# An LSTM's last steps and the attention after it: where one group's statistics and eight accumulating loads are issued

## The chip, the cores and the metric

The kernel runs on one core of one Trainium2 chip. The metric is the device time of one execution in microseconds (us). The engines are TensorE (PE in the profile), VectorE (DVE), ScalarE (ACT), GpSimd (POOL) and SyncE (SP), which here issues DMAs only.

## The reference

The input x is 128 batches of 64 nodes of 256 features, 8192 tokens in all. Four layers follow each other, and each adds its result to x:

```
for layer in (L0, L1, L2, L3):
    x = x + layer(relu(layernorm(x)))
L0: two graph convolutions with adj (64 x 64), then for p = 1..4 an LSTM over
    windows of p consecutive nodes; its last h replaces the window's last node
L1: attention with 4 heads of 64 over the 64 nodes of a batch, masked where adj == 0
L2: graph convolution, then linear, batchnorm, relu, linear, batchnorm
L3: three graph convolutions with adj * adj, 256 -> 512 -> 1024 -> 256
```

The change lies where L0 ends and L1 begins: `x = x + L0(...)`, the layer norm of the new x, and the first attention groups.

## The kernel before, in words

**Groups.** The tokens form NG = 16 groups of 512. The residual x of a group is a tile `xs[g]` of 128 partitions by 4 by 256 (512 KB). Groups 0 to 3 stay resident. Groups 4 to 7 and 8 to 11 are loaded from DRAM into memory that held the state of the LSTM, by `x_for(0)` and `x_for(1)` (L259, four loads each through `load_x`, L58, on SP's queue). Groups 12 to 15 are loaded in attention.

**The LSTM's state.** It is kept with features on the partitions, in four tiles `hs[0]` to `hs[3]` of 32 batches each, four groups to a tile. When a tile is final, `turn_nodes(part, room)` (L274) transposes a quarter of its nodes on VectorE (L278) and puts it down in DRAM (`ys`, L283, four DMAs on SP's queue). Then `add_turned(g)` (L287) adds a group's values to `xs[g]` with one accumulating DMA that POOL issues (L291).

**The last steps.** For window length p = 4 the units of work are taken in pairs; the pair at j = 2 is the last one. Each unit takes steps t = 1, 2, 3, and the two units alternate, so that there are six steps, and the code numbers them `slot` 0 to 5. A step (`next_step`, L677) makes four differences on VectorE (L685 to L690) and then two gate sets. A gate set (`seven`, L170) is a form of Strassen's scheme with seven products on PE (L568) in four PSUM banks: the results of the first two are copied by ScalarE (L179, L180) and summed by VectorE (L182, L183), POOL sums two of them (L187), VectorE makes the other outputs (L193, L197), and ScalarE applies the gates (L582). The step ends with the cell state (L699, L700), a tanh (L601) and the hidden state on VectorE (L603; in a unit's last step L609). `next_step` returns this last VectorE instruction, which the loop keeps as `stepped`.

Beside the six steps, both parts of `turn_nodes` for `hs[0]` and `hs[1]`, the accumulating loads listed for each slot in `ADDED_BESIDE` (L165), and `x_for` are issued. `summed_last()` is POOL's latest sum (L187); a load stands behind it on POOL.

**The first attention group.** At slot 4 the layer norm of group 0 is made as well: `ln_relu` makes statistics on VectorE (L92, L94, L95), a power on POOL (L96), the shift on VectorE (L98) and four activations on ScalarE (L111). Then `transposed` turns h on PE (L127) and `features` copies it (L302) and makes differences (L306, L310, L311).

**Attention.** For each group PE makes values (L901), the queries and keys in a scheme of seven products (L879, with POOL's sum at L187 again), transposes the exponentials of the group before (L962), attends (L975), transposes h of the next group (L127) and makes the scores (L926). `normalized(g + 2)` (L853) makes the layer norm of the group two ahead: statistics on VectorE (L860, L862), two operations on POOL (L864, L866). `add_output` (L983) adds the result of the group before the last to x on POOL (L990). In groups 1 to 3 and from 5 on, `add_turned` is called once in a group behind an operation that POOL made for a layer norm (`shifts_made`, L866).

**What sets the order.** A scheduler orders each engine's instructions by its own estimate of time, with program order as priority. `with tc.issue_after(ins)` puts the instructions of its block behind `ins` on the engine of `ins`; it is an order on that engine alone. Each engine runs its instructions in the order that results. The eight PSUM banks (`psp`) are taken in turn by all matmuls.

Of the kernel before, what the change touches and what calls it, by code (L numbers as in the profile page):

```python
# [24 lines left out]
NK = PER  # L25
# [13 lines left out]
def adj_preln_kernel(ctx: ExitStack, tc: tile.TileContext, x_in, adj, vec, bg0, bg1,  # L39
# [122 lines left out]
    HN = GN // 2  # L162

    sums_on_pool = []
    ADDED_BESIDE = ((), (), (0,), (1,), (2,), (3, 4))  # L165

    def summed_last():
        return sums_on_pool[-1]
# [90 lines left out]
    def x_for(i):  # L259

        four = hx.tile([P, PER, GT, D], F32, tag=f"h{i}", name=f"x_for_h{i}")
        for k in range(PER):
            xs.append(four[:, k])
            load_x(xs[-1], len(xs) - 1)
# [49 lines left out]
    with tc.tile_pool(name="lw", bufs=5) as lw:  # L314
# [220 lines left out]
        with tc.tile_pool(name="back", bufs=1, reuse_waits="tile") as back_pool, \  # L535
# [176 lines left out]
            def blocks_of(p, wi, wh):  # L712
# [14 lines left out]
                return ws, lambda: make([3])  # L727


            w0 = first_blocks(  # L730
                w_next[0], lw.tile([P, 2, 1024], F32, tag="w", name="s"), copied_of[5:9]
            )
            for p, nk in ((1, 8), (2, 8), (3, 7), (4, 8)):
                n = nk * HB
                wi, wh = w_next
                if p < 4:
                    w_next = (load_w(wih, p), load_w(whh, p))
                starts = range(0, NODES // p // nk * nk, nk)
                units = [(tiles, k0) for tiles in ((0, 1), (2, 3)) for k0 in starts]

                for j in range(0, len(units), 2):
                    two = [unit(p, *u, nk) for u in units[j : j + 2]]
                    first_steps(p, n, two, units[j : j + 2], w0)
                    if p > 1:
                        flush()
                        if j == 0:
                            ws, last_sum = blocks_of(p, wi, wh)
                    if j + 2 == len(units):
                        if p < 4:
                            w0 = first_blocks(  # L750
                                w_next[0], weight_tile(),
                                [copied_of[i] for i in (9, 14, 15, 15)] if p == 1 else None,
                            )
                        else:
                            w_att = weight_tile()
                            nc.sync.dma_start(
                                out=w_att[:, :, 0:768], in_=wqkv.rearrange("(c p) f -> p c f", p=P)
                            )
                            wqk = [[w_att[:, c, m * D : (m + 1) * D] for c in range(2)] for m in range(2)]
                            wv = w_att[:, :, 512:768]  # L760
                            ss = [w_att[:, c, 768:1024] for c in range(2)]
                            nc.vector.tensor_tensor(ss[0], wqk[1][0], wqk[1][1], ALU.add)
                            nc.vector.tensor_tensor(ss[1], ss[0], wqk[0][0], ALU.subtract)
                            nc.vector.tensor_tensor(wdiff, wqk[0][0], wqk[1][0], ALU.subtract)
                    for t in range(1, p):
                        for i, u in enumerate(two):
                            stepped = next_step(
                                t, p, n, u, ws, last_sum if (j, t, i) == (0, 1, 0) else None
                            )

                            if p == 4 and j == 2:
                                slot = 2 * t + i - 2
                                if slot == 0:
                                    room = keep.tile([P, 2, TN, 2, 32], F32, tag="arena", name="turned")
                                for part in range(2 * slot, min(2 * slot + 2, 8)):
                                    turn_nodes(
                                        part,
                                        room[:, part % 3] if part % 3 < 2 else back_pool.tile(
                                            [P, TN, 2, 32], F32, tag="hc", name="turned"
                                        ),  # L780
                                    )()
                                for x_of_group in ADDED_BESIDE[slot]:
                                    with tc.issue_after(summed_last()):
                                        add_turned(x_of_group)
                                if slot > 2:
                                    if slot < 5:
                                        x_for(slot - 3)
                            if p == 4 and j == 2 and t == p - 1 and i == 0:

                                h = back_pool.tile([P, GT, D], F32, tag="hc", name="h")  # L790
                                with tc.issue_after(stepped):
                                    ln_relu(xs[0], h)
                                hTs = keep.tile([P, 2, 2, GN], F32, tag="arena", name="hT")
                                hT = features(transposed(h))
# [55 lines left out]
    with tc.tile_pool(name="att", bufs=2, reuse_waits="tile") as ap_:  # L850
# [151 lines left out]
        for g in range(NG):  # L1002
            if g == NG - NK + 1:
                turn_pool.__exit__(None, None, None)
                hres_pool.__exit__(None, None, None)
                with tc.using_default_side("right"):
                    ar_right = ctx.enter_context(
                        tc.tile_pool(name="arena_r", bufs=NG // 2, reuse_waits="tile")
                    )
            hT_all, blocks = hT  # L1010
            v = ap_.tile([P, 2 * GT, P], F32, tag="v", name="v")
            moved = values(hT_all, v, (0,))
            if 0 <= g - NK < NK:
                with tc.issue_after(moved):
                    load_x(xs[g + 2 * NK], g + 2 * NK)
            q, k, finish = queries_keys(blocks)
            if g == 0:
                h = normalized(1)
            if last is not None:
                with tc.issue_after(finish.behind):  # L1020
                    if g > 1:
                        add_output(g - 2, pss, ri)
                    sums_of()
            if last is not None:
                e, ri, v_last = last
                if g > 1:
                    eT, turned = turn(e)
            added = finish()
            if g == NG - 1:

                w1 = w_att[:, :, 0:512]
                w2 = w_att[:, :, 512:1024].rearrange("p a (b f) -> a p b f", f=D)
                nc.sync.dma_start(out=w1, in_=w1t.rearrange("(c p) f -> p c f", p=P))
            moved = values(hT_all, v, (1,))
            if put_down:
                with tc.issue_after(moved):
                    put_down()
            put_down = None
            if g == 1:

                eT, turned = turn(e)
            if 0 < g <= NG - NK:
                with tc.issue_after(shifts_made[g]):
                    if g < 4:
                        add_turned(g + NK)
                    elif g > 4:
                        add_turned(g + NK - 1)
            if g + 1 < NG:
                hT = features(transposed(h))
            if g == 0:  # L1050

                with tc.issue_after(last_copy.ins):
                    nc.scalar.activation(rsum, mhalf[:, 0:1], AF.Exp)
            if g == NG - 1:
                turned_in = mixed(0, (on_scalar, on_scalar))
            if last is not None:
                pss = attend(eT, v_last)
            e_next = []

            def masked_scores():  # L1060
                e, masked = scores(q, k)
                e_next.append(e)
                return masked

            if g < NG - 1:
                masked_scores()
            else:
                with tc.issue_after(turned_in), tc.issue_after(added):
                    activated(ar_right, 1, masked_scores)
            ri_next, sub, sums_of = softmax(e_next[0])  # L1070
            last = (e_next[0], ri_next, v)
            with tc.issue_after(sub):
                if g < 8:
                    put_down = turn_nodes(
                        g + 8, tp.tile([P, TN, 2, 32], F32, tag="turned", name="turned")
                    )
                if g + 2 < NG:
                    h = normalized(g + 2)
                elif g + 2 == NG:
                    activated(ar_right, 0)  # L1080
# [587 lines left out]
```

## Time and profile before

| what | value |
|---|---|
| median of 3 runs (lowest to highest) | 2465.1 us (2464.9 to 2465.72) |
| the profiled execution, its own time | 2465.76 us |
| its span | 2464.0 us |
| mean granted clock of TensorE | 0.997 |
| PE busy | 2431.4 us (99%) |
| DVE busy | 1544.5 us (63%) |
| ACT busy | 1128.6 us (46%) |
| POOL busy | 463.3 us (19%) |

The time of an execution is a little more than its span, here by 1.76 us. Busy is the sum of an engine's instructions; an engine's idle time matters only where the work that ends last waits for it. In the timeline of this execution a step of the LSTM lasts 24.17 us on PE; slot 3 starts at 1133.08 us, slot 4 at 1157.25, the products of the last step at 1194.06, and attention at 1219.92.

### The profile page before, as it was taken

What the parts mean: (1) busy time and instruction counts of PE and PEld (TensorE: products, weight loads), DVE (VectorE), ACT (ScalarE), POOL (GpSimd) and SP (SyncE); (2) the same over time, 40 slices, a digit from 0 to 9 for tenths busy, and PEclk for the clock granted to TensorE, in tenths of its full rate; (3) what the DMA queues carried; (4) which work ended last, traced back from release to release, by engine and by line L of the source; (5) the groups of instructions that cost most, each with busy time, mean ns of one, the idle gap of its engine ahead of it and who ended that gap; (6) DMA issues with size and microseconds to landing.
All of it is one profiled execution on the core that took longest, in us unless ns stands there. A gap on an engine that the chain in (4) does not pass through costs nothing.

```text
span 2464.0 us, 46585 instructions
## 1 busy us (share of the span) xinstructions
PE 2431.4 (99%) x19564; PEld 2074.0 (84%) x19564; DVE 1544.5 (63%) x2768; ACT 1128.6 (46%) x2026; POOL 463.3 (19%) x400
## 2 busy tenths in 40 slices
PE   9999999999999999999899999999999999999999
PEld 6678888889999998888788864486888898898888
DVE  6668866666566565576499886476556455454544
ACT  4557754444354343343455566564333323333332
POOL 4431211111111111111134431023111111101110
PEclk9999999999999999999899999999999999999999
DMA  3200000001000000152257310010133100000000
GB/s 127 93 2 1 1 18 1 1 1 35 1 1 1 1 1 1 18 98 52 33 98 138 74 40 2 1 60 10 27 61 61 27 10 19 10 10 10 18 10 18
DMA packets 161587, 73.20 MB, mean 30 GB/s; under 512 B 104417, under 2 KB 157793, under 8 KB 161377
## 3 DMA queue, kind: packets, MB, share of 16 engines
q1 hardware_dynamic: 147712, 56.82, 9.3%
q0 software_dynamic: 12672, 12.58, 3.4%
q8 instruction: 154, 2.52, 0.4%
q10 hardware_dynamic: 992, 0.82, 0.1%
q14 instruction: 57, 0.46, 0.1%
HBM read 40.84 MB, written 20.97 MB: 25 GB/s over the span
## 4 chain that ended last, share of the span: by engine, by line
PE 88%; DVE 7%; ACT 3%; POOL 1%; issue 1%; DMA 0%; DVEq 0%; POOLq 0%; ACTq 0%
PE ps L568 41%; PE ps L1455 16%; PE ps L1503 8%; PE ps L829 4%; PE ps L144 4%; PE ps L1419 2%; PE ps L511 2%; PE ps L487 2%; PE ps L879 2%; PE ps L1211 2%; PE ps L1262 2%; PE ps L901 1%; ACT arena L237 1%; POOL arena L187 1%; DVE hT L306 1%
## 5 line engine op out<-in xcount | busy, mean ns | idle before, releaser
L568 PE MATMUL ps<-diff,s 128*128 128x256 f32 (+1 forms) x1824 | 393.5, 371 | 0.9 <-DVE diff L689 0.9
L1455 PE MATMUL ps<-arena 128*128 128x256 f32 x1792 | 392.4, 380 | 0.0
L1455 PEld LDWEIGHTS ps<-arena 128*128 128x128 f32 x1792 | 337.9, 190 | 53.9 <-issue 9.2
L568 PEld LDWEIGHTS ps<-diff,s 128*128 128x128 f32 x1824 | 346.1, 190 | 33.9 <-issue 1.6
L582 ACT ACTIVATE gates<-gates,lbias 128x512 f32<-128x512 f32 (+5 forms) x426 | 244.3, 621 | 203.8 <-DVE gates L193 146.0
L187 POOL TENSOR_TENSOR gates<-p 128x512 f32<-128x512 f32 (+1 forms) x115 | 149.2, 1297 | 892.5 <-DVE p L183 841.6
L568 PE MATMUL ps<-h,w 128*128 128x256 f32 (+1 forms) x1028 | 242.7, 373 | 0.0
L568 PE MATMUL ps<-diff,w 128*128 128x256 f32 (+1 forms) x1040 | 238.7, 370 | 0.0
L568 PEld LDWEIGHTS ps<-diff,w 128*128 128x128 f32 x1040 | 197.4, 190 | 18.2
L568 PEld LDWEIGHTS ps<-h,w 128*128 128x128 f32 x1028 | 196.2, 191 | 19.6 <-issue 0.5
L582 ACT ACTIVATE gates<-ps,lbias 128x256 f32<-128x256 f32 (+3 forms) x213 | 91.8, 477 | 249.2 <-PE ps L568 249.1
L187 POOL TENSOR_TENSOR arena<-arena 128x256 f32<-128x256 f32 (+1 forms) x73 | 81.8, 1120 | 580.4 <-DVE arena L183 550.7
L237 ACT ACTIVATE arena<-arena 128x512 f32<-128x512 f32 (+1 forms) x160 | 88.7, 582 | 186.9 <-POOL arena L187 94.6
L1503 PE MATMUL ps<-arena 128*128 128x128 f32 x1280 | 149.7, 276 | 0.0
L193 DVE TENSOR_TENSOR gates<-p,ps 128x512 f32<-128x512 f32 (+1 forms) x115 | 76.2, 663 | 114.4 <-PE ps L568 114.2
L1503 PEld LDWEIGHTS ps<-arena 128*128 128x128 f32 x1280 | 145.5, 192 | 1.1
L193 DVE TENSOR_TENSOR arena<-arena,ps 128x256 f32<-128x256 f32 (+1 forms) x73 | 43.5, 596 | 156.4 <-PE ps L1455 87.4
L182 DVE TENSOR_TENSOR p<-p,ps 128x512 f32<-128x512 f32 (+1 forms) x131 | 86.7, 662 | 53.9 <-PE ps L568 53.1
L568 PE MATMUL ps<-state,w 128*128 128x256 f32 (+1 forms) x512 | 116.1, 370 | 0.9 <-ACT p L179 0.8
L197 DVE TENSOR_TENSOR gates<-p,ps 128x512 f32<-128x512 f32 (+1 forms) x115 | 76.5, 666 | 64.4 <-PE ps L568 63.8
L568 PE MATMUL ps<-state,s 128*128 128x256 f32 (+1 forms) x512 | 115.8, 369 | 0.0
L829 PE MATMUL ps<-arena,w 128*128 128x512 f32 x256 | 114.3, 599 | 0.0
(207 smaller groups left out, 4027.4 us busy)
## 6 DMA issues: line engine op xcount, KB each, us to landing
x<-in_x SPq DMA_DIRECT2D x19, 512.0 KB, 5.4
y<-turned SPq DMA_DIRECT2D x64, 128.0 KB, 3.5
v<-vt SPq DMA_DIRECT2D x128, 64.0 KB, 2.5
w<-in_wih SPq DMA_DIRECT2D x4, 1024.0 KB, 8.5
x_for_h<-in_x SPq DMA_DIRECT2D x8, 512.0 KB, 9.2
x<-y POOLq DMA_DIRECT2D x8, 512.0 KB, 6.4
x_for_h<-y POOLq DMA_DIRECT2D x8, 512.0 KB, 6.5
z<-w SPq DMA_DIRECT2D x64, 64.0 KB, 2.0
```

The source lines that it names most:

```text
L144: last = nc.tensor.matmul(pss[b][half * 64 : half * 64 + 64, c, t, :], lhsT=src[rows, t, col : col + 64], rhs=a2[rows, :], start=True, sto ...
L182: nc.vector.tensor_tensor(p1, p1, ps[2], ALU.add)
L187: nc.gpsimd.tensor_tensor(out=out[1][1], in0=p1, in1=p5, op=ALU.add).ins
L193: nc.vector.tensor_tensor(out[0][1], p1, ps[1], ALU.add)
L197: last = nc.vector.tensor_tensor(to, p, q, ALU.add)
L237: nc.scalar.activation(o, o, func)
L487: nc.tensor.matmul(ps[:, t, :], lhsT=m0[:, c, tok : tok + P], rhs=wg[0][:, c, :], start=(c == 0), stop=(c == 1),)
L568: nc.tensor.matmul(ps[:, r], lhsT=wc[:, j, :], rhs=bc, start=first and r == 0 and c == 0, stop=True, skip_group_check=True,)
L582: nc.scalar.activation(o, ps, func, bias=lbias[:, col : col + 1])
L829: nc.tensor.matmul(ps, lhsT=w1[:, c, m * P : (m + 1) * P], rhs=a[:, 2 + c, :], start=(c == 0), stop=(c == 1),)
L1455: nc.tensor.matmul(ps[:, r, :], lhsT=w[:, c, col : col + P], rhs=b[:, c, :], start=first and r == 0 and c == 0, stop=c == 1, skip_group_ch ...
L1503: nc.tensor.matmul(ps[:, t, :], lhsT=w[:, c, t * P : (t + 1) * P], rhs=b[:, c, :], start=first and t == 0 and c == 0, stop=c == 3, skip_gr ...
```

## The change

It has three parts. The statistics of the first attention group are put behind the last VectorE instruction of the step before (`stepped_before`, slot 3) instead of that of slot 4. The accumulating loads of groups 0 to 7 are listed in pairs beside slots 2 to 5; before, groups 0, 1 and 2 were listed one by one beside slots 2 to 4, groups 3 and 4 beside slot 5, and groups 5 to 7 were loaded in attention groups 1 to 3. And `x_for(0)` and `x_for(1)` are called at slots 2 and 3 instead of 3 and 4.

```diff
-    ADDED_BESIDE = ((), (), (0,), (1,), (2,), (3, 4))
+    ADDED_BESIDE = ((), (), (0, 1), (2, 3), (4, 5), (6, 7))
...
+            stepped = None
...
                         for i, u in enumerate(two):
+                            stepped_before = stepped
                             stepped = next_step(
...
                                 for x_of_group in ADDED_BESIDE[slot]:
                                     with tc.issue_after(summed_last()):
                                         add_turned(x_of_group)
-                                if slot > 2:
-                                    if slot < 5:
-                                        x_for(slot - 3)
+                                if slot in (2, 3):
+                                    x_for(slot - 2)
                             if p == 4 and j == 2 and t == p - 1 and i == 0:
...
-                                with tc.issue_after(stepped):
+                                with tc.issue_after(stepped_before):
                                     ln_relu(xs[0], h)
...
             if 0 < g <= NG - NK:
                 with tc.issue_after(shifts_made[g]):
-                    if g < 4:
-                        add_turned(g + NK)
-                    elif g > 4:
+                    if g > 4:
                         add_turned(g + NK - 1)
```

## The prediction

> **What bounds the kernel now.** I read the page first, then the chain of waits around the change, then each engine's timeline from 1100 to 1350 us, then a table of stretches. The page says that TensorE works nearly all the time, so only the places where it stands still can give time back; the clock row shows one weak slice, the 20th, which is 1170 to 1232 us.
>
> ```profile
> PE 2431.4 (99%) x19564; PEld 2074.0 (84%) x19564; DVE 1544.5 (63%) x2768; ACT 1128.6 (46%) x2026; POOL 463.3 (19%) x400
> PEclk9999999999999999999899999999999999999999
> ```
>
> The timeline of PE there shows the hole. Columns: start, length, line, operands, count, and in brackets the idle time before it and its releaser.
>
> ```profile
> 1179.69 1.89 PE L568 MATMUL ps<-diff,w 128*128 128x256 f32 x8
> 1192.10 2.16 PE L127 MATMUL ps<-ident,h 128*128 128x128 f32 x8 [10.52 <-ACT h L111]
> 1194.06 3.58 PE L568 MATMUL ps<-h,w 128*128 128x256 f32 x8
> ...
> 1229.42 1.04 PE L127 MATMUL ps<-ident,h 128*128 128x128 f32 x8
> ```
>
> The last products of step five of six (slot 4 in the code) are issued by 1181.42 (1179.69 and eight at 0.216 us, the spacing of every full run of eight). PE's next instructions are the transposes of the first attention group's h, ahead of the last step's products, and they wait 10.52 us. They then take 1.96 us start to start instead of 1.03, and the eight after them 3.41 instead of 1.73. The other engines show why h is late:
>
> ```profile
> 1186.82 1.29 DVE L609 TENSOR_TENSOR h<-gates 128x512 f32<-128x512 f32 x2 [1.18 <-ACT gates L601]
> 1188.04 1.40 DVE L92 BATCH_NORM_STATS2 st<-x 128x6 f32<-128x256 f32 x4
> ...
> 1190.18 1.04 POOL L96 TENSOR_TENSOR rstd<-rstd,mhalf 128x4 f32<-128x4 f32 x1 [10.35 <-DVE rstd L95]
> ...
> 1191.45 2.07 ACT L111 ACTIVATE h<-x,nmr,rstd 128x256 f32<-128x256 f32 x4 [4.66 <-DVE nmr L98]
> ```
>
> The statistics (L92) start exactly when slot 4's last VectorE instruction (L609) is done. Data does not hold them: the accumulating load of xs[0] was issued at 1130.21 us and such a load lands 5.9 to 8.7 us after issue, by 1140. It is the order that the old tie asks for.
>
> A second, smaller loss lies in attention. For groups 2 and 4 (POOL, DVE, PE, then POOL and DVE):
>
> ```profile
> 1256.08 1.32 POOL L291 DMA_DIRECT2D x_for_h<-y  x1
> 1256.92 3.01 POOL L990 TENSOR_TENSOR x<-x,o 128x512 f32<-128x512 f32 x2
> 1259.40 1.75 POOL L187 TENSOR_TENSOR k<-p 128x512 f32<-128x512 f32 x1
> ...
> 1259.69 2.02 DVE L306 TENSOR_TENSOR hT<-hT 128x512 f32<-128x512 f32 x1 [0.81 <-ACT hT L302]
> ...
> 1261.21 0.69 PE L926 MATMUL ps<-k,q 64*64 64x64 f32 x32 [0.67 <-POOL k L187]
> ...
> 1286.38 1.28 POOL L187 TENSOR_TENSOR k<-p 128x512 f32<-128x512 f32 x1
> ...
> 1290.07 0.69 DVE L306 TENSOR_TENSOR hT<-hT 128x512 f32<-128x512 f32 x1 [0.81 <-ACT hT L302]
> ```
>
> With an accumulating load (L291) ahead of them, POOL's sums come about 3 us later, meet L306 and stretch it from 0.69 to 2.02, and PE waits for k. The table of stretches cuts attention at each group's first values matmul; columns after the stretch are its length and each engine's busy time:
>
> ```profile
> 1246.53:1261.83 15.30, 14.15 (x193) 11.94 (x188) 14.31 (x29) 8.06 (x14) 6.32 (x6) 1.00 0.66 116
> 1261.83:1277.03 15.20, 14.16 (x195) 11.94 (x189) 14.26 (x28) 8.06 (x14) 6.33 (x6) 1.00 0.61 106
> 1277.03:1291.31 14.28, 13.92 (x194) 11.84 (x189) 13.30 (x29) 8.06 (x14) 4.95 (x5) 1.00 0.53 110
> 1291.31:1305.14 13.83, 13.81 (x194) 11.90 (x189) 12.90 (x28) 7.96 (x14) 6.10 (x6) 1.00 0.56 116
> ```
>
> These are groups 2 to 5. Groups 2 and 3 have the load in front; group 4 has none, but starts late; group 5 has it behind POOL's sums and is bound by PE alone: 13.83.
>
> **What the Trainium skill says.** "TensorE: Matmul & The Clock Gate", section "What's actually happening": an idle window of about 3.4 us halves PE's clock, and about as much work restores it. The trace agrees: after 10.52 us idle, the next 5.37 us hold work that takes 2.70 at full pace, and the granted clock of 1181.42 to 1194.06 is 0.59. "SBUF — State Buffer", section "Who interferes with whom": a VectorE instruction with two SBUF inputs and a GpSimd one that reads SBUF lock each other out. L306 at 2.02 beside L187, and 0.69 without, agrees. "DMA: Bandwidth & Descriptors", section "SWDGE vs HWDGE vs iDMA": accumulating transfers go only through GpSimd, which writes their descriptors. Agrees: each costs POOL 1.3 us.
>
> **The change, part by part.**
>
> *The tie.* The statistics may start after slot 3's last VectorE instruction (L603, over at 1163.88) instead of slot 4's (1188.1). From first L92 to last L111 takes 1188.04 to 1193.52, 5.5 us. Now VectorE has slot 4's own work around it (4.7 us between 1163.79 and 1168.5) and ScalarE is busy 9.33 of the 24.17 us; with 4.7 and 4 us added h is ready by about 1178, before 1181.42. VectorE is busy 13.57 us of that slot, so 2.0 us of statistics fit. Saved: the last step then starts at 1181.42 + 0.97 (eight transposes at full clock, as at 1360.92) = 1182.39, lasts 24.17 as slot 4 does, and attention's first matmul comes at 1206.56 instead of 1219.92: **13.36 us**. What is late next: nothing; slot 5's differences (L685 to L690) were done by 1168, and of the eight PSUM banks the last of slot 4's second gate set is free at 1182.31 (L197), while the product that may need it comes 5.2 us into the step.
>
> *The new wait.* L98 on VectorE waits for POOL's power (L96), 0.83 us in the trace. Behind it could stand slot 4's L183, which ended at 1165.68 and frees a bank that PE uses again at 1167.61. Four L92, the rest and the wait could make it 3 us late, PE 1 us; if the order puts L183 first, nothing. Not shown by the trace: 0 to 1.5 us lost, a gain excluded. I take 0, since a wait behind ready work is the likelier order.
>
> *Pairs of loads.* L291 is added once in each of slots 2, 3 and 4, none in slot 5, and gone from groups 1 to 3: eight in either kernel. A pair in slot 5 took POOL from 1216.98 to 1219.61, and POOL idles some 10 us before each L187 of these steps; VectorE's L193 inside that pair took its usual 0.69. Cost nothing, hidden by POOL's idle time; without that cover, 1.3 us each. DMA is busy 0.12 to 0.15 there. The pair with xs[0] lands by about 1144, 20 us before use.
>
> *SP's queue.* The two groups of four loads (L58) come one slot earlier in the text. Today they run at 1100.0 to 1108.8, behind 21 puts, and land by 1119.5. If four of them pass eight puts, y[1] is complete 5 us later, about 1111; loads 4 and 5 are issued at 1178. Nothing. Bounds: 0 either way.
>
> *Attention.* Group 1 (14.99 us) has its waits for VectorE and ScalarE, not POOL's sum: 0. Group 2 keeps its late start and becomes like group 4: 15.30 to 14.28, 1.02. Groups 3 and 4 become like group 5: 1.37 and 0.45. Together **2.84 us**. Bounds: 0, if another wait takes over, and 4.0, if group 1 also falls to 13.83.
>
> Sum: 13.36 + 2.84 = 16.2 us. The profiled execution has a span of 2464.0 and 1.76 around it (2465.76); 2465.76 - 16.2 = 2449.56, and it lies 0.66 above the median of the runs, so 2448.9: I say **2449.0**.
>
> **The rivals.**
> *Attention gives nothing* (0.14): VectorE is busy 14.3 of group 2's 15.3 us, so another of its waits may take over. Against it: groups 4 and 5 run the same work without the load in front. Time 2451.7.
> *h is still late* (0.08): PE works in order; if the transposes stand between slot 4's two gate sets (1169.34), h, ready at 1169.4 to 1178, stalls PE 4 us at mid value, and 2.8 us of slow clock follow. Time 2465.1 - 16.2 + 6.8 = 2455.7.
> *The tie was not the cause* (0.05): the statistics stay where they were, for instance because the order on VectorE puts them behind slot 4's gate work anyway. Against it: VectorE stood idle five times in that slot. Time 2462 to 2465.
> *Slower* (0.03): POOL stands at slot 4's pair waiting for x or y to land. Behind it is slot 5's L187, normally 8.6 us into the step (slot 4: 1165.83 after 1157.25); ScalarE's L582 needs its result at 1195.5 and holds the copies that free PE's banks. A block beyond 1194 costs PE microsecond for microsecond, and beyond 1210 eats the whole gain; to 1222 it gives 2477. Against it: those inputs are there by 1120.
>
> **How the numbers follow.** The forecast has 0.70, with a range of its own of 2446 to 2453 (from 1.2 us more in attention and some noise, to 1.5 lost at the new wait and half of the attention gain). The range of 2446 to 2456.5 adds the first two rivals. A measurement can tell 0.2%, 4.9 us, from no change: the forecast and the first two rivals are faster, 0.92; the third is within, 0.05; slower 0.03.
>
> **What would show it.** PE's idle time before the L127 in the steps goes from 10.52 to under 1 us; the eight L568 after it take 1.9, not 3.58; L92 starts near 1164 to 1168; the slice's clock is 9. In groups 2 and 3 L306 takes 0.69 and no L291 stands between L866 and L187; their lengths are 14.3 and 13.8. Four pairs of L291 follow L187 in slots 2 to 5. Wrong would be an idle PE of several microseconds anywhere from 1157 to 1207, or an L187 in slots 4 or 5 that waits for an L291.

## The result, and the profile after

| what | before | after |
|---|---|---|
| median of 6 runs (lowest to highest) | 2465.19 us (2464.62 to 2466.4) | 2450.06 us (2449.65 to 2452.14) |
| the profiled execution, its own time | 2465.76 us | 2449.65 us |
| its span | 2464.0 us | 2447.9 us |
| slot 4's first product to attention's first values matmul | 62.67 us | 49.22 us |
| from there to the last group's attend | 239.75 us | 237.04 us |

The ratio of the times is 0.994, with a 95% interval of 0.9927 to 0.9953, which lies below 1: the changed kernel is faster, by 15.1 us in the medians and 16.1 us between the two profiled executions. In a later measurement, of five runs, the changed kernel's median was 2449.54 us beside 2465.59 us of the kernel before (ratio 0.9935, 0.9923 to 0.9948). In the table, "to the last group's attend" means to the start of its products.

The page after has no weak slice left in the clock row, and PE's busy time fell by 3.3 us although it ran the same number of instructions. About 2.7 us of that is the work after the hole, which ran at half pace before; the other 0.7 us lies in attention groups 2 to 4 (14.15, 14.16 and 13.92 us busy before, 13.92, 13.82 and 13.82 after).

```profile
PE 2428.1 (99%) x19564; PEld 2072.4 (85%) x19564; DVE 1540.7 (63%) x2768; ACT 1127.7 (46%) x2026; POOL 464.0 (19%) x400
PEclk9999999999999999999999999999999999999999
```

The timeline of PE at the place of the hole (the line numbers from attention on are higher by one in the changed kernel):

```profile
1179.47 1.89 PE L568 MATMUL ps<-diff,w 128*128 128x256 f32 x8
1181.20 1.04 PE L127 MATMUL ps<-ident,h 128*128 128x128 f32 x8
1182.07 1.89 PE L568 MATMUL ps<-h,w 128*128 128x256 f32 x8
```

No bracket stands at L127, so it waits for nothing, and the eight products after it take 1.73 us start to start, not 3.41. The other engines in slot 4, from the timelines of DVE, POOL and ACT:

```profile
1162.43 1.23 DVE L603 TENSOR_TENSOR state<-gates 128x1024 f32<-128x1024 f32 x1 [1.18 <-ACT gates L601]
...
1164.17 0.42 DVE L92 BATCH_NORM_STATS2 st<-x 128x6 f32<-128x256 f32 x1
1164.51 0.67 DVE L183 TENSOR_TENSOR p<-p,ps 128x512 f32<-128x512 f32 x1
1165.10 1.07 DVE L92 BATCH_NORM_STATS2 st<-x 128x6 f32<-128x256 f32 x3
...
1168.76 0.16 DVE L98 SCALAR_TENSOR_TENSOR nmr<-mv,rstd 128x4 f32<-128x4 f32 x1 [0.94 <-POOL rstd L96]
...
1178.27 2.62 POOL L291 DMA_DIRECT2D x_for_h<-y  x2
...
1170.76 1.08 ACT L111 ACTIVATE h<-x,nmr,rstd 128x256 f32<-128x256 f32 x2
```

The statistics start with L603's end; L183, which frees a bank of PE's, stands between the first L92 and the other three and ends at 1165.18; L98 waits 0.94 us for POOL, and no wait of PE follows from it; h is complete at 1171.84, 9.4 us before PE wants it. In attention, the timelines of POOL and DVE in group 2:

```profile
1242.27 1.27 POOL L187 TENSOR_TENSOR k<-p 128x512 f32<-128x512 f32 x1
1243.50 2.54 POOL L991 TENSOR_TENSOR x<-x,o 128x512 f32<-128x512 f32 x2
...
1245.96 0.69 DVE L306 TENSOR_TENSOR hT<-hT 128x512 f32<-128x512 f32 x1 [0.73 <-ACT hT L302]
```

And the table of stretches for groups 2 to 5. Its columns are the stretch, its length, the busy time (and instructions) of PE, of PE's weight loads, DVE, ACT and POOL, the granted clock, the share of the DMA engines and GB/s:

```profile
1232.87:1247.21 14.34, 13.92 (x194) 11.81 (x189) 13.40 (x30) 8.07 (x14) 4.93 (x5) 1.00 0.41 74
1247.21:1261.05 13.84, 13.82 (x195) 11.90 (x189) 12.91 (x28) 7.96 (x14) 4.92 (x5) 1.00 0.43 78
1261.05:1274.89 13.84, 13.82 (x194) 11.90 (x189) 12.90 (x28) 7.97 (x14) 4.92 (x5) 1.00 0.54 111
1274.89:1288.72 13.83, 13.81 (x194) 11.90 (x189) 12.90 (x28) 7.96 (x14) 6.10 (x6) 1.00 0.56 120
```

With no load ahead of it POOL's sum of k is early, L306 takes 0.69 us, and groups 3 and 4 have come down to group 5's length, which PE alone sets.

### The profile page after: what moved, and what is told of

It is laid out like the page before. It is cut to its first block, busy times and chain, and to the rows that moved or that the text cites. A ratio compares the mean times of both kernels' runs of the same rounds, so it can differ in the third digit from the quotient of the medians.

```text
span 2447.9 us, 46580 instructions
## 1 busy us (share of the span) xinstructions
PE 2428.1 (99%) x19564; PEld 2072.4 (85%) x19564; DVE 1540.7 (63%) x2768; ACT 1127.7 (46%) x2026; POOL 464.0 (19%) x400
## 4 chain that ended last, share of the span: by engine, by line
PE 90%; DVE 6%; ACT 2%; POOL 1%; issue 1%; DVEq 0%; POOLq 0%; ACTq 0%
PE ps L568 41%; PE ps L1454 16%; PE ps L1502 8%; PE ps L830 4%; PE ps L144 4%; PE ps L880 3%; PE ps L1418 2%; PE ps L511 2%; PE ps L487 2%; PE ps L1210 2%; PE ps L1261 2%; PE ps L902 1%; ACT arena L237 1%; POOL arena L187 1%; PE ps L963 1%
## 5 line engine op out<-in xcount | busy, mean ns | idle before, releaser
L568 PE MATMUL ps<-diff,s 128*128 128x256 f32 (+1 forms) x1824 | 393.5, 371 | 0.9 <-DVE diff L689 0.9
L568 PEld LDWEIGHTS ps<-diff,s 128*128 128x128 f32 x1824 | 345.9, 190 | 33.8 <-issue 1.6
L568 PE MATMUL ps<-h,w 128*128 128x256 f32 (+1 forms) x1028 | 241.0, 371 | 0.0
L568 PE MATMUL ps<-diff,w 128*128 128x256 f32 (+1 forms) x1040 | 238.7, 370 | 0.0
L568 PEld LDWEIGHTS ps<-diff,w 128*128 128x128 f32 x1040 | 197.4, 190 | 18.2
L568 PEld LDWEIGHTS ps<-h,w 128*128 128x128 f32 x1028 | 195.0, 190 | 19.2 <-issue 0.5
L568 PE MATMUL ps<-state,w 128*128 128x256 f32 (+1 forms) x512 | 116.1, 370 | 0.9 <-ACT p L179 0.8
L197 DVE TENSOR_TENSOR gates<-p,ps 128x512 f32<-128x512 f32 (+1 forms) x115 | 76.6, 666 | 63.3 <-PE ps L568 62.7
L568 PE MATMUL ps<-state,s 128*128 128x256 f32 (+1 forms) x512 | 115.8, 369 | 0.0
```

The lines of the kernel that those rows point to most:

```text
L197: last = nc.vector.tensor_tensor(to, p, q, ALU.add)
L568: nc.tensor.matmul(ps[:, r], lhsT=wc[:, j, :], rhs=bc, start=first and r == 0 and c == 0, stop=True, skip_group_check=True,)
```

## The experiments

The theory: two separate gains. The old tie held h back while PE, whose order is the same in both kernels, stood before its transposes; and the loads stood ahead of POOL's sums in attention. Total times of one kernel differ by 0.3 to 4.9 us from run to run (2.5 us for the changed kernel in its first six runs). The profiles show one source of such differences: in some of them PE's granted clock is lower in the first 30 us or near 1450 us (0.78 in the first 15 us of the kernel with the tie alone, 0.94 from 1440 to 1470 us in the kernel with the loads behind POOL's sums), where the changed kernel's profile has 1.00. That this makes up the whole spread is not shown, since each kernel has one profile. So the stretches inside a profile are compared, and the totals only beside them. "Steps" is slot 4's first product to attention's first values matmul, "attention" from there to the last group's attend. Line numbers differ by a few from kernel to kernel.

### One part alone, two kernels

The tie alone (with the two lines that make `stepped_before`):

```diff
 # the kernel before, with
...
-                                with tc.issue_after(stepped):
+                                with tc.issue_after(stepped_before):
```

> The kernel before with the tie alone moved (statistics of group 0 behind slot 3's last VectorE instruction); the loads stay where they were. Theory (two separate gains): the hole on PE goes as in the changed kernel, 13.4 us, and attention keeps its loss: 2451.7 us, PE idle before the transposes under 0.5 us, attention groups 2, 3 and 4 at 15.3, 15.2 and 14.3 us. Rival (the loads in pairs are what lets the statistics run early, or the two parts need each other): h stays late, 2460 us or more.

Measured: 2453.55 us (2452.77 to 2454.16; ratio 0.9949, 0.9937 to 0.9962). Steps 49.22 us, exactly as in the changed kernel; attention 239.67, as before. The total is 1.9 us above what was expected. The kernel before, measured beside it, had a median of 2466.0 us, 0.8 above its earlier one; and in the profiled execution all that comes before slot 4 took 1.15 us longer than in the kernel before, with a granted clock of 0.78 in the first 15 us against 1.00.

The loads alone:

```diff
 # the changed kernel, with
-                                with tc.issue_after(stepped_before):
+                                with tc.issue_after(stepped):
```

> The changed kernel with the old tie (statistics behind slot 4's last VectorE instruction). Theory: the hole stays with its 10.5 us and the slow clock after it; groups 2, 3 and 4 take 14.3, 13.8 and 13.8 us; gain 2.7 us, 2462.4 us. Rival (removing the loads from attention gives nothing, another wait takes over): 2465 us. Second rival (the loads were the cause of the hole): near 2450 us.

Measured: 2462.96 us (2461.81 to 2464.96; ratio 0.9988, 0.9981 to 0.9994). Steps 62.88 us, attention 237.05. PE's timeline still has the hole:

```profile
1192.69 2.16 PE L127 MATMUL ps<-ident,h 128*128 128x128 f32 x8 [10.52 <-ACT h L111]
1194.65 3.62 PE L568 MATMUL ps<-h,w 128*128 128x256 f32 x8
```

What follows: each part gives its own gain without the other, 13.45 and 2.7 us, and they add. All three rivals fall. PE, VectorE and ScalarE run their instructions in the same order in this kernel as in the kernel before; only the orders on POOL and SP differ, so the gain in attention comes from there. The steps of the kernel with the tie alone last as long as those of the changed kernel, so the pairs of loads cost nothing in them.

### The loads of x at their old slots

```diff
 # the changed kernel, with
-                                if slot in (2, 3):
-                                    x_for(slot - 2)
+                                if slot in (3, 4):
+                                    x_for(slot - 3)
```

> The changed kernel with the loads of x for groups 4 to 11 called at slots 3 and 4 as before; only SP's order of loads and puts differs. Theory (this part costs and gives nothing): within 0.5 us of the changed kernel, 2450 us. Rival (the earlier calls are needed, so that slot 4's pair finds its x): POOL waits at slot 4's pair and the time grows, 2452 us or more.

Measured: 2449.58 us (2449.39 to 2450.41; ratio 0.9934, 0.9922 to 0.9947), steps 49.22, attention 236.94. In the traces this kernel's order differs from the changed kernel's on SP alone, and the difference costs nothing.

### No tie, and a tie in the middle

```diff
 # the changed kernel, with
-                                with tc.issue_after(stepped_before):
+                                with nullcontext():
```

> The changed kernel with no tie at all on group 0's statistics: VectorE's order then has the first L92 in slot 2, right after the accumulating load of x was issued (about 1130 us), while PE's order is unchanged. Theory (engines run in order, so a statistics instruction that waits for a landing holds the gate work behind it): VectorE waits some 5 us for the landing, L182 and L183 of slot 3 come late, PE waits 3 to 5 us for banks: 2453 to 2456 us. Rival (VectorE's idle time in the steps hides it): 2450 us, as the changed kernel.

Measured: 2454.65 us (2452.46 to 2456.43; ratio 0.9953, 0.9939 to 0.9967). From the timelines of DVE and PE:

```profile
1137.10 0.75 DVE L92 BATCH_NORM_STATS2 st<-x 128x6 f32<-128x256 f32 x2 [3.94 <-DMA x<-y]
1137.77 0.67 DVE L197 TENSOR_TENSOR gates<-p,ps 128x512 f32<-128x512 f32 x1
...
1146.67 3.19 PE L568 MATMUL ps<-diff,w 128*128 128x256 f32 x8 [2.15 <-DVE p L183]
```

And two rows of the table of stretches, one at the start of slot 3 and one after PE's wait; the granted clock is the third value from the end:

```profile
1133.96:1144.36 10.40, 10.40 (x49) 8.94 (x48) 6.43 (x18) 3.85 (x7) 1.04 (x1) 1.00 0.60 95
1146.67:1150.08 3.41, 3.40 (x9) 2.72 (x10) 3.41 (x8) 0.13 (x1) 1.58 (x1) 0.59 0.00 0
```

VectorE stands 3.94 us at the first statistics instruction for the load's landing, with L197 behind it; the delay runs through the next step's L183 to PE's bank. Slot 3 takes 28.28 us (1134.00 to 1162.28) instead of 24.17: some 2.3 us by the wait and the rest in the 16 products behind it, most of them at the slow clock. So the tie earns its place: here a statistics instruction that VectorE reached before its data was paid for by the gates.

The tie in the middle of slot 4:

```diff
 # the changed kernel, with
+        set_added.append(added.ins)       # in seven(): L183 of each gate set
...
-                                with tc.issue_after(stepped_before):
+                                with tc.issue_after(set_added[-1]):
```

> The changed kernel with the statistics tied in the middle: behind the second L183 of slot 4's second gate set (over at about 1177 us). Theory (h is late by as much as the tie is, and PE pays for it one to one beyond its own end of slot 4 at 1181.2): h is ready about 1183 to 1186, PE stands still for 2 to 5 us, and slot 4's start to attention takes 51 to 55 us instead of 49.2; more by up to 2.8 if the clock falls. Rival (any tie before slot 4's end would do): 49.2 us.

Measured: 2451.57 us (2451.29 to 2451.92; ratio 0.9945, 0.9932 to 0.9958), steps 51.01 us, 1.79 more than the changed kernel. On PE (the products, L568 elsewhere, are L570 here):

```profile
1183.44 0.44 PE L127 MATMUL ps<-ident,h 128*128 128x128 f32 x2 [1.51 <-ACT h L111]
1183.72 0.60 PE L570 MATMUL ps<-h,w 128*128 128x256 f32 x2
```

That is the lower end of what was expected for the steps, and PE stands still for less than the 2 to 5 us expected. h is complete at 1186.10, at the late end of what was expected, but PE does not pay for this one to one: the scheduler splits the transposes here, two at a time between products, so PE waits only for the first quarter of h. That part of the theory did not hold. The other part did: a tie late in the slot costs time, so not any tie before the slot's end would do.

### The share of the clock

```diff
 # the kernel before, with
...
+                                filled = bank((P, 2, 256)).rearrange("p a b -> p (a b)")
+                                with tc.issue_after(issued[0]):       # slot 4's last product
+                                    for _ in range(22):
+                                        last = nc.tensor.matmul(
+                                            filled[:, 0:256], lhsT=ident, rhs=wdiff, start=True, stop=True
+                                        )
-                                hT = features(transposed(h))
+                                with tc.issue_after(last.ins):
+                                    hT = features(transposed(h))
```

> The kernel before with 22 extra matmuls of 128x128 by 128x256 (their result is used by nothing) on PE between slot 4's last product and the waiting transposes, about 9.5 of the 10.5 us. Theory (2.8 of the 13.4 us are slow clock): PE's pace stays full, the transposes and the eight products after them take 0.97 and 1.73 us, and the stretch from slot 4's start to attention falls from 62.67 to 59.9 us; total 2462.3 us. Rival (the slow pace after the hole has another cause, such as the ScalarE or VectorE work beside it): 62.7 us, total as before.

Measured: 2468.14 us (2466.65 to 2471.57; ratio 1.0013, 1.0006 to 1.0019), so the total was missed by 5.8 us. The steps are nearly as expected: 60.35 us, 2.32 less. In this kernel the extra matmuls are L800, the transposes L127 as before, and the scores L936:

```profile
1180.92 9.66 PE L800 MATMUL ps<-wdiff,ident 128*128 128x256 f32 x44
1191.61 0.93 PE L127 MATMUL ps<-ident,h 128*128 128x128 f32 x4 [1.02 <-ACT h L111]
...
1405.25 0.45 PE L936 MATMUL ps<-k,q 64*64 64x64 f32 x12 [2.32 <-issue]
...
1448.79 0.21 PE L936 MATMUL ps<-k,q 64*64 64x64 f32 x1 [2.03 <-issue]
```

With PE kept at work the transposes and the first eight products take 3.05 us (1191.61 to 1194.66) instead of 5.37: the slow pace did come from the standstill. The total is lost in attention, 244.49 us against 239.75: the last two lines show PE standing 2.32 and 2.03 us for nothing that the profile shows, at places where the kernel before has no such stop. The 22 matmuls (44 records in the trace) moved all later ones in PE's stream, and their result takes one turn of the PSUM banks. Both stops end 1.3 to 1.4 us after a 16 KB transfer of the DMA queue for instructions (1402.88 to 1403.83 and 1445.94 to 1447.49 us), so PE may have waited for its instructions; but 28 other such transfers between 1150 and 1500 us pass without such a stop. That is a hint, and the cause stays open.

### The place of the loads on POOL

The loads of groups 5 to 7 left in attention, behind POOL's sums (`added_on_pool` is a list of add_output's sums on POOL, L990):

```diff
 # the kernel with the tie alone, with
-                with tc.issue_after(shifts_made[g]):
+                with tc.issue_after(
+                    shifts_made[g] if g > 4 else added_on_pool[-1] if g > 1 else summed_last()
+                ):
```

> The kernel with the tie alone, and the loads of groups 5 to 7 left in attention groups 1 to 3, but issued behind POOL's sum of k and behind its two sums of add_output instead of behind the layer norm's operation. Theory (it is the load's place ahead of POOL's sums that costs, not the load): from attention's first values matmul to the last group's attend 237.0 us, as in the changed kernel, against 239.75 in the kernel before; total as the changed kernel. Rival (the loads' own time on POOL or on the DMA engines costs): 239 us or more.

Measured: 2450.24 us (2449.37 to 2451.4; ratio 0.9939, 0.9925 to 0.9953), attention 237.06 us. POOL in group 2:

```profile
1242.51 1.27 POOL L187 TENSOR_TENSOR k<-p 128x512 f32<-128x512 f32 x1
1243.73 2.52 POOL L995 TENSOR_TENSOR x<-x,o 128x512 f32<-128x512 f32 x2
1246.19 1.30 POOL L291 DMA_DIRECT2D x_for_h<-y  x1
```

The same loads in the same groups, and all of attention's gain is there. So what cost 2.7 us went with their place on POOL, and not with their own 1.3 us there nor their traffic.

One thing is not separated by this. When the load moved, the order of the sums changed too. In groups 2 and 3 of the kernel before, POOL runs the load, then add_output's two sums, then the sum of k; here and in the changed kernel it runs the sum of k first and add_output's sums after it. In group 2 the sum of k starts 12.87 us after the group's start in the kernel before and 9.40 us in the changed kernel. Of these 3.47 us the load takes 0.84, start to start, and add_output's sums take 2.48. PE was ready for k about 14.0 us after the group's start, and without the load k is done at 10.67. An estimate from these numbers: the load alone ahead of k would not have made PE wait, and add_output's sums ahead of k did. Group 1 fits this: the load stands ahead of k there without add_output's sums, and the group takes 14.99 us with it and 15.00 without, though it has other waits. A kernel with the load ahead and the sum of k still first was not run, so how much is the load's own doing and how much that of the changed order of the sums stays open.

Then the same for groups 8 to 15, which the change had left as they were:

```diff
 # the changed kernel, with
+        LOADED_IN = {g: () for g in range(NG)}
+        LOADED_IN.update({5: (8, 9), 6: (10,), 7: (11,), 9: (12, 13), 10: (14,), 11: (15,)})
...
-                with tc.issue_after(shifts_made[g]):
-                    if g > 4:
-                        add_turned(g + NK - 1)
+                with tc.issue_after(added_on_pool[-1] if g > 4 else shifts_made[g]):
+                    for i in LOADED_IN[g]:
+                        add_turned(i)
```

> The changed kernel with the loads of groups 8 to 15, too, issued behind POOL's sums of k and of add_output (two in groups 5 and 9, one in groups 6, 7, 10 and 11). Theory (place on POOL): groups 6 to 8 fall from about 14.7 to 15.1 us to 13.9, and from attention's first values matmul to the last attend it takes 233 to 234 us instead of 237.0; total 3 to 4 us under the changed kernel, 2446.5 us. Rival (a load that is later by some 5 us makes the statistics of its group wait on VectorE): 237 us or more.

Measured: 2445.54 us (2445.46 to 2449.83; ratio 0.9926, 0.9912 to 0.994), attention 233.14 us. Groups 6 to 9 take 13.85, 13.87, 14.13 and 13.60 us instead of 14.68, 15.10, 15.10 and 13.89. In groups 6 to 8 the sum of k, which stood behind the load and add_output's sums in the changed kernel, comes first here; group 8 has no load of its own in this kernel. So this result repeats the one before it, with the same thing left open.

### Batches of four, and the best version beside the changed kernel

```diff
 # the changed kernel, with
-    ADDED_BESIDE = ((), (), (0, 1), (2, 3), (4, 5), (6, 7))
+    ADDED_BESIDE = ((), (), (0, 1, 2, 3), (), (4, 5, 6, 7), ())
```

> The changed kernel itself, as the measure for the two runs beside it. Both theories: 2450 us; slot 4's start to attention 49.2 us, attention 237.0 us.

> The changed kernel with the eight loads in two batches of four, beside slots 2 and 4 (POOL then works some 5.2 us on end at each, 1130 to 1135 and 1178 to 1183). Theory (a load costs nothing while POOL would idle until its next sum): within 0.5 us of the changed kernel, slot 2 to attention unchanged. Rival (the cost is there but too small to see with two): PE waits in slot 3 or 5, 1 to 3 us more.

> The version with all attention loads behind POOL's sums once more, on the same chip as the changed kernel, to settle the difference between the two. Theory: attention 233.1 us against 237.0, total 3.9 us under the changed kernel. Rival (the earlier difference of totals came from different chips or from the clock at the kernel's start): less than 2 us.

Measured, on one chip: the changed kernel 2449.54 us (2449.46 to 2449.72); batches of four 2450.09 (2449.58 to 2451.74; ratio to before 0.9938, 0.9926 to 0.9951), steps 49.23 and attention 236.97; the best version 2445.8 (2444.92 to 2447.55; ratio to before 0.992, 0.9907 to 0.9934), steps 49.22 and attention 233.18. POOL with four loads, in slots 2 and 4, and its next sums:

```profile
1130.41 5.42 POOL L291 DMA_DIRECT2D x<-y  x4
1141.86 1.58 POOL L187 TENSOR_TENSOR gates<-p 128x512 f32<-128x512 f32 x1 [6.03 <-DVE p L183]
...
1178.69 5.25 POOL L291 DMA_DIRECT2D x_for_h<-y  x4
1190.45 1.26 POOL L187 TENSOR_TENSOR gates<-p 128x512 f32<-128x512 f32 x1 [6.51 <-DVE p L183]
```

Even four in a row leave POOL 6 us idle before its next sum, so a pair costs nothing there. The best version is 3.7 us under the changed kernel in the medians and 3.8 us shorter in attention; the rival of chips and clocks falls.

## Why the prediction was right, point by point

**The tie.** Forecast 13.36 us, measured 13.45 (62.67 to 49.22). The step that sized it, that the last step starts one set of transposes after slot 4, held; the transposes took 0.87 us, not 0.97. (The 1.03 us that the prediction sets beside 1.96 is a length of the profile and not a time from start to start; the sum uses 0.97.) h was complete at 1171.84 and not by about 1178: what the other work on VectorE and ScalarE would add was put too high, which changed nothing, since PE needs h only at 1181.20. The clock's part, which the sum held without naming, is confirmed by the filler: 2.32 of the 2.67 us of slow pace came back, and in the rest PE waited for the later parts of h, which ScalarE finished between 1191.6 and 1193.0.

**The new wait.** L98's wait was 0.94 us, and it cost nothing, the value taken. The reason given held in its order: L183 was placed ahead of three of the four L92. The kernel without a tie shows what a longer wait of VectorE can do: there it stood 3.94 us for a load's landing, not for POOL, and slot 3 took 4.1 us longer.

**Pairs and SP's queue.** Nothing each, as taken; the tie-alone kernel's steps, the batches of four and the loads of x at their old slots show it directly. No sum of POOL in slots 4 and 5 waits for a load.

**Attention.** Forecast 2.84 us, measured 2.71. By groups: group 1 0 (15.00 after 14.99), group 2 0.96 for 1.02, group 3 1.36 for 1.37, group 4 0.44 for 0.45. That the place on POOL matters, and not the load as such, is shown by the kernel that left the loads in attention behind the sums. The prediction puts the whole delay of some 3 us down to the load ahead of the sums; 2.5 us of it are add_output's sums, which had changed places with the sum of k. The sizes came from groups 4 and 5, which have neither the load nor the changed order in front, so they came out right whichever of the two it is.

**The sum.** 16.2 forecast, 16.1 between the profiled spans: 13.45 and 2.71, 0.22 ahead of slot 4 and 0.28 lost after attention. The forecast of 2449.0 lies 1.06 below the first median and 0.5 below the later one. The term that was off is the last: the 0.66 us by which the profiled execution lay above the median was taken off as if it were the kernel's; the changed kernel's profiled execution lies 0.41 below its median instead. Such a difference from run to run belongs in the range and not in the sum.

**The rivals.** That attention gives nothing, that h is still late and that the tie was not the cause are all excluded by the tie-alone and loads-alone kernels. That POOL blocks at slot 4's pair did not occur in any kernel here; a pair that really waits for its inputs was not tried, so its price is not shown.

## What to carry to other kernels

When an engine stands still, look at what stands next in its queue: PE had slot 5's products at hand and waited for eight transposes placed ahead of them, so a cheap chain on three other engines, tied one step too late, cost 13.45 us. A tie is a place between two ends: too late and the consumer waits, too early and the engine stops at data that has not landed, with everyone else's work behind it. And an instruction in a queue has a price by what stands behind it and in which order: with the same 1.3 us load ahead of POOL's sums, and add_output's sums ahead of k, a group took up to 1.4 us longer; with the load behind the sums it cost nothing.

## What the runs showed of the hardware that was not expected

The length of a PE wait did not alone decide whether its clock fell. A wait of 2.15 us (no tie) was followed by 3.41 us at a mean granted clock of 0.59, although it is shorter than the idle window of about 3.4 us that the prediction names. A wait of 2.32 us (extra matmuls) left the clock at 1.00 in the 4 us from 1405 on, and one of 1.51 us (tie in the middle) left it at 1.00 as well. A wait of 1.09 us on ScalarE behind attention was followed by a clock of 0.52 from 1454 to 1456 us in the kernel with the loads behind POOL's sums; the same wait in the changed kernel was followed by 1.00. What decides it is not shown. After the hole the way back took longer than the prediction's "about as much work": 5.37 us of work passed before full pace.

And 22 more matmuls on PE brought two stops of 2.32 and 2.03 us, for nothing that the profile shows, more than 200 us after the place where they were added.
